# Graph attention and a graph convolution on one core: checks moved into the convolution, an end in written order, and outputs stored a block at a time

## The chip, the cores and the metric

The kernel runs on one core of one Trainium2 chip. The metric is the device time of one execution in microseconds. All data is in float32; some operands of TensorE are rounded to its own 32-bit form (fp32r).

## The reference, cut to what matters

```python
n, d = x.shape                      # 2708, 128
h = 8
q, k, v = ((x @ W.T).reshape(d, n, h) for W in (Wq, Wk, Wv))
a = jnp.einsum('dnh,dmh->dnm', q, k) * d ** -0.5
a = softmax(a + adj + adj, axis=2)
o = jnp.einsum('dnm,dmh->dnh', a, v).reshape(n, h * d) @ Wo.T
x = layernorm(x + o)
local_hidden = adj @ (x @ W2) + b2
local_cross = adj @ (local_hidden @ W4) + b4
embed = local_cross + local_hidden @ res_w.T + res_b
return layernorm(x + embed)
```

There are 128 heads of 8 channels over the same 2708 × 2708 matrix adj, so the attention has by far the most work. The layer normalisations are over the 128 features of a row and have no weights.

## The kernel before, in words

**Start and projections.** The first 256 rows of x and all three projection weights are loaded, and project_all makes the first queries, keys and values. The projections of the other rows are made in "quarters" that are strewn through the attention: load_quarter (L334, L336) loads a chunk of x (xc) and a quarter of a weight (wc), project (L344) multiplies them and hands the rest on as small jobs. The first of them, load_quarter(0), stands at L407, behind the first projections and the loads of the first group.

**Attention.** 32 groups of four heads; in a group six blocks of 452 query columns (the last has 448); in a block nine steps. A step makes scores on TensorE (L438), adds adj to most of them on VectorE (L445, tile e) and takes the exponential on ScalarE (L537). For one chunk of rows in each step the adjacency is not added ahead of the exponential: ScalarE takes the exponential of the bare scores (L534, tile w), and GpSimd multiplies it by exp(2·adj) (L535, tile ecol). exp(2·adj) is made once, in the first group, by first_exp: L418 on ScalarE, with accum_out, which sums each row beside the exponential, and L420 stores it to the buffers ne; later groups load it from there. In the last three groups look_at_near (L427) takes a minimum of each such tile. The products with the values add up in PSUM (L455, L460, L463); hand_on copies a block's sums out (L469) and stores them (L471, buffer os). The order of these steps on TensorE is written out by interleave, a planner with costs of its own for each step; loads run up to eight tiles ahead on SP's queue.

There is no maximum taken off before the exponentials. In its place the kernel checks that sums and factors lie within bounds, counts the partitions where they do in n_fine, and reads that number at the end; if a partition doesn't, a second form of the attention is run.

**End, first pass (layer0_out).** The weights and biases of the end are loaded first (L544 to L551). Then, for each of 22 chunks of 128 rows (the last has 20): load the head sums (ot, L587) and rows of x (xt, L589), two chunks ahead, in three buffers; reciprocal of the softmax sums (rd, L595); minimum and maximum of the sums for the check (reach, L598); product of all eight heads' sums with rd on VectorE (on, L600); eight transposes (pt, L603), a copy on ScalarE (oT, L605), eight products with Wo (py, L611), plus x (ys, L615), and mean and variance (statistics, L567 and L568). The chunks are taken in written order, with divide one chunk ahead of project and two ahead of add_x.

**End, second pass.** One root over the deviations of all chunks (L630), a reciprocal (L631), and then, four chunks at a time, normalise (L639), transpose (px, L641), copy (L646), multiply by W2 (pw, L649) and copy to xw (L651). The checks follow (L654 to L667).

**Layer 1.** Two passes over adj in six blocks of columns (five of 512 and one of 148), 22 tiles to a block. propagate loads a tile (col, L679, SP's queue, 24 buffers) and adds its product up in PSUM (acc, L680). In the first pass the sum plus b2 is lhT (L688), whose chunks are multiplied by W4 (ph, L691) and copied to hw (L692). In the second, a product with res_w is added (L683), the bias too (eT, L697), and for each chunk of 128 rows: transpose (pe, L700), plus x1 (y, L702), statistics, root, reciprocal, normalise (L574 to L577, tile xo), store (L705). This part has no written order: a scheduler decides where the instructions of one block stand among the loads and products of the next.

All loads and stores named here are issued by SP, in one order.

Of the kernel before, what the change touches and what calls it, by code (L numbers as in the profile page):

```python
# [18 lines left out]
P = 128  # L19
# [11 lines left out]
NEAR_LOW = 1e-30  # L31
NEAR_HIGH = 1e18
# [110 lines left out]
def graph_attention_gcn(ctx: ExitStack, tc: tile.TileContext, x, xT, adj, adjT, adjP, adjS,  # L143
# [42 lines left out]
    ends = const.tile([P, 2, len(QBS) * len(TWO_EXP)], F32, name="ends")  # L186


    with ExitStack() as s:
# [184 lines left out]
        for n in range(2):  # L374
            load_adj(n)

# [30 lines left out]
        load_quarter(0)  # L407
# [5 lines left out]
        def first_exp(b, m):  # L413

            nw = QBS[b][1]
            t = ecols.tile([P, QB], F32, tag="ecol", name="ecol")
            x = b * len(TWO_EXP) + TWO_EXP.index(m)
            nc.scalar.activation(t[:, :nw], adj_cols[0, b, -1 - m][:, :nw], AF.Exp, scale=2.0,  # L418
                                 accum_out=ends[:, 1, x : x + 1])
            nc.sync.dma_start(near_exp[b, m][:, :nw], t[:, :nw])  # L420
            exp_cols[0, b, m] = t

        def look_at_near(g, b, m):

            x = TWO_EXP.index(m)
            if x % 3 == g - NG + 3:
                nc.vector.tensor_reduce(ends[:, 0, ds(b * len(TWO_EXP) + x, 1)], exp_cols[g, b, m][:, : QBS[b][1]],  # L427
                                        AX.X, ALU.min)
# [51 lines left out]
        for what, n, c, beside in interleave(plan, len(steps) // len(plan), NU, amid, bufs=5):  # L480
# [14 lines left out]
            if c == 1 and jobs:  # L495
                jobs.pop(0)()
            if c == 0:
# [34 lines left out]
            if c == len(pieces) - 1:  # L532
                look_at_near(g, b, two)
                nc.scalar.activation(w[:, :, :nw], sp[:, :, :nw], AF.Exp, scale=2.0)  # L534
                nc.gpsimd.tensor_mul(w[:, :, :nw], w[:, :, :nw],  # L535
                                     exp_cols[g, b, two][:, :nw].unsqueeze(1).to_broadcast([P, 3, nw]))
                nc.scalar.activation(e[:, :at, :nw], e[:, :at, :nw], AF.Exp, scale=2.0)  # L537
# [5 lines left out]
    wo = keep.tile([P, H, D], F32, name="wo")  # L543
    nc.sync.dma_start(wo.rearrange("g e f -> g (e f)"), WoT)  # L544
    w2, w4, rw = (keep.tile([P, P], F32, name=f"w{i}") for i in range(3))
    for t, src in ((w2, W2), (w4, W4), (rw, res_wT)):
        nc.sync.dma_start(t, src)
    b2_sb, b4_sb, rb_sb, bias = (keep.tile([P, 1], F32, name=f"b{i}") for i in range(4))
    for t, src in ((b2_sb, b2), (b4_sb, b4), (rb_sb, res_b)):
        nc.sync.dma_start(t, src)  # L550
    nc.vector.tensor_add(bias, b4_sb, rb_sb)  # L551

# [8 lines left out]
    reach = keep.tile([P, 2, NM], F32, name="reach")  # L561
    nc.gpsimd.memset(reach, 1.0)
    fine = keep.tile([P, 5], F32, name="fine")
# [6 lines left out]
    def layernorm(to, y, w):  # L570
        mv = stat.tile([P, nc.vector.BN_AGGR_DIM], F32, tag="mv", name="mv")
        statistics(mv[:w], y, w)
        sd = stat.tile([P, 1], F32, tag="sd", name="sd")
        nc.scalar.activation(sd[:w], mv[:w, 1:2], AF.Sqrt, bias=eps[:w])  # L574
        rs = stat.tile([P, 1], F32, tag="rs", name="rs")
        nc.vector.reciprocal(rs[:w], sd[:w])
        nc.vector.tensor_scalar(to, y, mv[:w, 0:1], rs[:w], ALU.subtract, ALU.mult)  # L577

    def layer0_out(sb, ps, pa, judge):
# [4 lines left out]
        def load(c):  # L584
            i0, w = MC[c]
            ot = sb.tile([P, H + 1, P], F32, tag="ot", name="ot")
            nc.sync.dma_start(ot[:w], o3[ds(i0, w)])  # L587
            xt = sb.tile([P, D], F32, tag="xt", name="xt")
            nc.sync.dma_start(xt[:w], x[ds(i0, w), :])  # L589
            given[c] = ot, xt  # L590

        def divide(c):
# [3 lines left out]
            if judge:  # L596
                for i, op in enumerate((ALU.min, ALU.max)):
                    nc.vector.tensor_reduce(reach[:w, i, c : c + 1], ot[:w, H, :], AX.X, op)  # L598
            on = sb.tile([P, H, P], F32, tag="on", name="on")
            nc.vector.tensor_mul(on[:w], ot[:w, :H, :], rd[:w].unsqueeze(1).to_broadcast([w, H, P]))  # L600
# [16 lines left out]

        load(0)
        load(1)
        for c in range(NM + 2):  # L620
            if c + 2 < NM:
                load(c + 2)
# [4 lines left out]
            if c >= 2:  # L627
                add_x(c - 2)
        sd, rs = (sb.tile([P, NM], F32, tag=n, name=n) for n in ("sds", "rss"))
        nc.scalar.activation(sd, mvs[:, :, 1], AF.Sqrt, bias=eps)  # L630
        nc.vector.reciprocal(rs, sd)  # L631
        for c0 in range(0, NM, 4):
            cs = range(c0, min(c0 + 4, NM))
            px = pa.tile([P, 4, P], F32, tag="px", name="px")
            x1T = sb.tile([P, 4, P], F32, tag="x1T", name="x1T")
            pw = pa.tile([P, 4, P], F32, tag="pw", name="pw")
            for c in cs:
                w = MC[c][1]
                nc.vector.tensor_scalar(x1[:w, c, :], ys[:w, c, :], mvs[:w, c, 0:1], rs[:w, c : c + 1],  # L639
                                        ALU.subtract, ALU.mult)  # L640
                nc.tensor.transpose(px[:, c - c0, :w], x1[:w, c, :], ident[:w, :w])  # L641

            full = len([c for c in cs if MC[c][1] == P])
            parts = [(0, full, P)] + [(c - c0, 1, MC[c][1]) for c in cs if MC[c][1] < P]
            for i, n, w in parts:
                nc.scalar.copy(x1T[:, ds(i, n), :w], px[:, ds(i, n), :w])  # L646
            for c in cs:
                w = MC[c][1]
                nc.tensor.matmul(pw[:w, c - c0, :], x1T[:, c - c0, :w], w2, start=True, stop=True)  # L649
            for i, n, w in parts:  # L650
                nc.scalar.copy(xw[:w, ds(c0 + i, n), :], pw[:w, ds(i, n), :])  # L651
        if judge:
            finite = sb.tile([P, NM * D], F32, tag="finite", name="finite", bufs=1)
            nc.vector.tensor_scalar(finite, ys.rearrange("p c f -> p (c f)"), 0.0, 0.0, ALU.mult, ALU.is_equal)  # L654
            nc.vector.tensor_reduce(fine[:, 0:1], finite, AX.X, ALU.min)
            bounds = [(reach[:, 0, :], ALU.min, SUM_LOW, ALU.is_ge), (reach[:, 1, :], ALU.max, SUM_HIGH, ALU.is_le)]
            bounds += [(ends[:, 0, :], ALU.min, NEAR_LOW, ALU.is_ge), (ends[:, 1, :], ALU.max, NEAR_HIGH, ALU.is_le)]
            for i, (a, way, limit, op) in enumerate(bounds):
                end = keep.tile([P, 1], F32, name=f"end{i}")
                nc.vector.tensor_reduce(end, a, AX.X, way)  # L660
                nc.vector.tensor_scalar(fine[:, 1 + i : 2 + i], end, limit, None, op)
            every, ones = (keep.tile([P, 1], F32, name=n) for n in ("every", "ones"))
            nc.vector.tensor_reduce(every, fine, AX.X, ALU.min)
            nc.gpsimd.memset(ones, 1.0)
            pf = pa.tile([P, NB], F32, tag="py", name="pf", bufs=2)
            nc.tensor.matmul(pf[:1, :1], every, ones, start=True, stop=True)
            nc.vector.tensor_copy(n_fine, pf[:1, :1])  # L667

    def layer1(s, cols):
# [4 lines left out]
        def propagate(src, n0, nw, last=None):  # L674

            acc = ps.tile([P, NB], F32, tag="wide", name="acc1")
            for m, (m0, mw) in enumerate(MC):
                t = cols.tile([P, NB], F32, tag="col", name="col1")
                nc.sync.dma_start(t[:mw, :nw], adjT[ds(m0, mw), ds(n0, nw)])  # L679
                nc.tensor.matmul(acc[:, :nw], src[:mw, m, :], t[:mw, :nw], start=(m == 0),  # L680
                                 stop=(last is None and m == NM - 1))
            if last is not None:
# [3 lines left out]
        for n0, nw in NBS:  # L686
            acc = propagate(xw, n0, nw)
            nc.vector.tensor_scalar(lhT[:, ds(n0, nw)], acc[:, :nw], b2_sb, None, ALU.add)  # L688
            for i, w in chunks(nw, P):
# [4 lines left out]
        for n0, nw in NBS:  # L694
            acc = propagate(hw, n0, nw, (rw, lhT[:, ds(n0, nw)]))
            eT = sb.tile([P, NB], F32, tag="eT", name="eT")
            nc.vector.tensor_scalar(eT[:, :nw], acc[:, :nw], bias, None, ALU.add)  # L697
            for i, w in chunks(nw, P):
                pe = pa.tile([P, NB], F32, tag="narrow", name="pe")
                nc.tensor.transpose(pe[:w, :D], eT[:, ds(i, w)], ident)  # L700
                y = sb.tile([P, D], F32, tag="y", name="y1")
                nc.vector.tensor_add(y[:w], pe[:w, :D], x1[:w, (n0 + i) // P, :])  # L702
                o = sb.tile([P, D], F32, tag="xo", name="xo")
                layernorm(o[:w], y[:w], w)
                nc.sync.dma_start(out[ds(n0 + i, w), :], o[:w])  # L705

    def rest(judge):
        with ExitStack() as s:
            cols = s.enter_context(tc.tile_pool(name="cols1", bufs=24))
            with ExitStack() as t:  # L710
# [3 lines left out]
                t.enter_context(tc.manual_schedule())  # L714
                layer0_out(sb, ps, pa, judge)
            layer1(s, cols)
# [136 lines left out]
```

## Time and profile before

| | us |
|---|---|
| median of 3 runs | 6884.85 (6881.82 to 6886.79) |
| profiled execution | 6884.26 |
| its span | 6882.5 |
| start and projections | 0 to 62 |
| attention | 62 to 6543, some 201.5 for a group |
| end, first pass | 6543 to 6642.3 |
| end, second pass | 6642.3 to 6661.6 |
| layer 1, first pass | 6661.6 to 6764 |
| layer 1, second pass | 6764 to 6874.4 |
| tail | 6874.4 to 6882.5 |
| busy PE, DVE, ACT, POOL | 97%, 89%, 95%, 84% of the span |
| DMA | 1674 MB, 243 GB/s on average |

The profile is one execution of the program, with times from the start of its span; 1.8 us of the execution's own time lie outside the span. A row of the timeline gives the start, the time that it took, the engine, the line of the code, the operation, what it writes and reads, shapes and the number of instructions; in brackets stands how long the engine was idle before it and what it waited for. SPq, ACTq and so on are the instructions with which an engine issues a DMA. PE is TensorE's multiplication and PEld its loading of weights; DVE is VectorE, ACT ScalarE, POOL GpSimd.

### The profile page before, as it was taken

Reading aid. Unit: us, or ns where it says so; the run is one execution under the profiler, and the core shown is the slowest. Engines: PE = TensorE matmul, PEld = TensorE weight load, DVE = VectorE, ACT = ScalarE, POOL = GpSimd, SP = SyncE. Lnnn points to the kernel's source line nnn. Section 1 sums busy time; section 2 is a strip of 40 time slices with the busy share of each in tenths; the row PEclk is TensorE's granted clock in tenths of the full one; section 3 lists DMA queues with packets and bytes.
Section 4 is the critical chain, followed back from the end, with each engine's and each line's share of the span. In section 5 each row is a group of like instructions: output and inputs, shape, how many; then the busy total and the mean of one; then the engine's idle time right before and its main releaser. Section 6 shows DMA issues by size and latency. Waiting matters only on the chain.

```text
span 6882.5 us, 138849 instructions
## 1 busy us (share of the span) xinstructions
PE 6655.3 (97%) x50666; PEld 2002.7 (29%) x50666; DVE 6106.7 (89%) x6373; ACT 6505.4 (95%) x3659; POOL 5789.3 (84%) x2706
## 2 busy tenths in 40 slices
PE   7999999999999999999999999999999999999979
PEld 2222222222222222222222222222222222222254
DVE  6899999999999999999999999999999999999941
ACT  7999999999999999999999999999999999999910
POOL 5899988989888899998889999889898898888800
PEclk8999999999999999999999999999999999999999
DMA  8888888778888877788887778887788878777667
GB/s 254 261 250 250 249 244 248 243 246 250 249 254 245 239 245 244 246 251 252 246 243 248 244 240 250 242 253 243 248 251 247 249 233 239 243 233 230 193 204 233
DMA packets 1168590, 1674.27 MB, mean 243 GB/s; under 512 B 153982, under 2 KB 1135954, under 8 KB 1163802
## 3 DMA queue, kind: packets, MB, share of 16 engines
q1 hardware_dynamic: 1167642, 1664.50, 79.0%
q8 instruction: 402, 6.59, 0.4%
q14 instruction: 290, 2.38, 0.1%
q10 hardware_dynamic: 256, 0.81, 0.1%
HBM read 1582.90 MB, written 81.80 MB: 242 GB/s over the span
## 4 chain that ended last, share of the span: by engine, by line
PE 58%; DMA 11%; DVE 11%; POOL 6%; issue 5%; ACT 5%; SPq 4%; DVEq 0%; ACTq 0%; POOLq 0%
PE acc L463 29%; PE s L438 18%; DVE e L445 10%; POOL w L535 6%; DMA col<-in_adjP 4%; PE acc L680 3%; DMA two<-in_adjP 3%; ACT e L537 3%; PE p L438 2%; PE acc L455 2%; SPq L287 2%; ACT w L534 2%; DMA ecol<-ne 2%; PE s L344 1%; PE acc L460 1%
## 5 line engine op out<-in xcount | busy, mean ns | idle before, releaser
L535 POOL TENSOR_TENSOR w<-w,ecol 128x1356 f32<-128x1356 f32 (+1 forms) x1728 | 5347.8, 3102 | 696.1 <-ACT w L534 601.6
L445 DVE TENSOR_TENSOR e<-s,col 128x904 f32<-128x904 f32 (+1 forms) x4608 | 4817.2, 1091 | 320.6 <-PE s L438 130.3
L537 ACT ACTIVATE e<-e 128x2712 f32<-128x2712 f32 (+5 forms) x1728 | 4593.8, 2658 | 9.3 <-DVE e L445 4.3
L463 PE MATMUL acc<-e,vals 128*9 128x452 f32 x20352 | 3561.9, 545 | 0.4 <-ACT e L537 0.4
L438 PE MATMUL s<-q,k 32*128 32x452 f32 x10944 | 2475.2, 462 | 120.9 <-DVE e L445 93.3
L534 ACT ACTIVATE w<-p 128x1356 f32<-128x1356 f32 (+1 forms) x1728 | 2286.0, 1323 | 33.9 <-PE p L438 20.4
L438 PEld LDWEIGHTS s<-q,k 32*128 32x128 f32 x10944 | 997.6, 182 | 3267.6 <-DVE e L445 2845.5
L463 PE MATMUL acc<-w,vals 128*9 128x452 f32 x10368 | 1622.0, 544 | 0.0
L438 PE MATMUL p<-q,k 32*128 32x452 f32 (+1 forms) x5184 | 1328.1, 444 | 21.2 <-ACT w L534 19.6
L445 DVE TENSOR_TENSOR e<-s,two 128x904 f32<-128x904 f32 (+1 forms) x960 | 1048.3, 1092 | 126.5 <-PE s L438 81.3
L463 PEld LDWEIGHTS acc<-e,vals 128*9 128x9 f32 x20352 | 441.7, 88 | 786.2 <-issue 773.7
L438 PEld LDWEIGHTS p<-q,k 32*128 32x128 f32 x5184 | 547.1, 182 | 51.0 <-ACT w L534 45.3
L463 PEld LDWEIGHTS acc<-w,vals 128*9 128x9 f32 x10368 | 207.0, 88 | 175.8 <-issue 160.3
L262 POOL CAST k<-k_raw 128x336 fp32r<-128x336 f32 x251 | 222.2, 886 | 30.1 <-DMA q<-qs 30.1
L460 PE MATMUL acc<-e,v_first 128*32 128x452 f32 (+1 forms) x1536 | 188.9, 564 | 9.8 <-DVE o L469 2.0
L455 PE MATMUL acc<-e,v_short 128*128 128x452 f32 (+1 forms) x384 | 195.1, 590 | 0.0
L344 PE MATMUL s<-wc,xc 128*128 128x256 f32 (+1 forms) x480 | 166.4, 428 | 8.9 <-DMA wc<-in_WkT 7.5
L469 DVE COPY o<-acc 128x452 f32<-128x452 f32 x192 | 119.9, 624 | 40.0 <-PE acc L463 39.8
L360 POOL TENSOR_TENSOR pr<-pa,pr 128x256 fp32r<-128x256 f32 (+1 forms) x160 | 117.8, 736 | 12.8
L346 DVE TENSOR_SCALAR pa<-s 128x256 f32<-128x256 f32 (+1 forms) x240 | 100.2, 418 | 27.6 <-PE s L344 23.9
L344 PEld LDWEIGHTS s<-wc,xc 128*128 128x128 f32 (+1 forms) x480 | 70.5, 184 | 133.4 <-DVE e L445 116.4
L680 PE MATMUL acc<-col,xw 128*128 128x512 f32 (+2 forms) x264 | 106.0, 551 | 0.0
(85 smaller groups left out, 1041.6 us busy)
## 6 DMA issues: line engine op xcount, KB each, us to landing
col<-in_adjP SPq DMA_DIRECT2D x1965, 226.0 KB
two<-in_adjP SPq DMA_DIRECT2D x1440, 226.0 KB
ecol<-ne SPq DMA_DIRECT2D x1395, 226.0 KB
col<-in_adjP SPq DMA_DIRECT2D x393, 224.0 KB
two<-in_adjP SPq DMA_DIRECT2D x288, 224.0 KB
ecol<-ne SPq DMA_DIRECT2D x279, 224.0 KB
col<-in_adjT SPq DMA_DIRECT2D x210, 256.0 KB
k_raw<-ks SPq DMA_DIRECT2D x504, 84.6 KB
```

The source lines that it names most:

```text
L262: copy(k[:, :, ts(i, n)], t[:, ts(i, n * NU)].rearrange("p (q c) -> p c q", c=NU))
L287: queues[i].dma_start(q[ds(32 * j + 2 * H * i, 2 * H), :nw].bitcast(F32), qs[:, ds((GB * g + j) * N + n0, nw)])
L344: nc.tensor.matmul(pp[:mi, 0, :QW], given[c][:, :mi], given.pop((c, i, h)), start=True, stop=True)
L438: nc.tensor.matmul(to[:, :nw], k[r, m, :], q[r], start=True, stop=True)
L445: nc.vector.tensor_add(e[:, ds(at, 2), :nw], st[:, :, :nw], a)
L455: nc.tensor.matmul(a[:, :nw], vz, e[:, t, :nw], start=False, stop=False)
L460: nc.tensor.matmul(a[ds(32 * j, 32), :nw], v_first[g % 2][:, ds(32 * j, 32)], e[:, t, :nw], start=True, stop=False)
L463: nc.tensor.matmul(a[ds(32 * j, VW), :nw], v[:, m, ds(VW * j, VW)], e[:, t, :nw], start=False, stop=(m == last_chunk))
L534: nc.scalar.activation(w[:, :, :nw], sp[:, :, :nw], AF.Exp, scale=2.0)
L535: nc.gpsimd.tensor_mul(w[:, :, :nw], w[:, :, :nw], exp_cols[g, b, two][:, :nw].unsqueeze(1).to_broadcast([P, 3, nw]))
L537: nc.scalar.activation(e[:, :at, :nw], e[:, :at, :nw], AF.Exp, scale=2.0)
L680: nc.tensor.matmul(acc[:, :nw], src[:mw, m, :], t[:mw, :nw], start=(m == 0), stop=(last is None and m == NM - 1))
```

## The change

- load_quarter(0) moves to the first loads of the kernel.
- first_exp loses accum_out, and look_at_near goes. The check on the factors is made on adj itself: in the first pass of layer 1 VectorE takes the largest absolute value of each tile (132 of them).
- The weights wo, w2 and the biases are loaded 40 steps before the attention's end; w4 and rw after the first three loads of the end.
- layer0_out: ot has four buffers and xt six, loads run three chunks ahead; the reach reductions go; the product "on" is split, five heads on VectorE and three on GpSimd; roots, normalisation, transposes and the product with W2 are made for four chunks at a time within the pass.
- All of the end is in written order (manual_schedule). In it the work that follows a block (form_hw; put_out) is kept in a list and taken when the next block has loaded its tile 3 or 6.
- The checks (verdict) are made in block 0 of the second pass of layer 1, at its tile 6, from the stored sums (os, loaded once more) and the largest values; their count at tile 3 of block 1.
- Outputs: a block's four chunks are transposed into one PSUM tile, with one sum y, one root, one reciprocal, four normalisations and one store. Of block 0 this is done at tile 6 of block 1, of the others at tile 3 of the next block.

The diff, cut to its core:

```diff
@@ -373,6 +383,7 @@
         for n in range(2):
             load_adj(n)
+        load_quarter(0)
...
             project_all(1, i)()
-        load_quarter(0)
...
-            nc.scalar.activation(t[:, :nw], adj_cols[0, b, -1 - m][:, :nw], AF.Exp, scale=2.0,
-                                 accum_out=ends[:, 1, x : x + 1])
+            nc.scalar.activation(t[:, :nw], adj_cols[0, b, -1 - m][:, :nw], AF.Exp, scale=2.0)
...
+            if n == len(steps) - 40 and c == 0:
+                load_weights()
...
-                look_at_near(g, b, two)
...
-            ot = sb.tile([P, H + 1, P], F32, tag="ot", name="ot")
+            ot = sb.tile([P, H + 1, P], F32, tag="ot", name="ot", bufs=4)
...
-            if judge:
-                for i, op in enumerate((ALU.min, ALU.max)):
-                    nc.vector.tensor_reduce(reach[:w, i, c : c + 1], ot[:w, H, :], AX.X, op)
             on = sb.tile([P, H, P], F32, tag="on", name="on")
-            nc.vector.tensor_mul(on[:w], ot[:w, :H, :], rd[:w].unsqueeze(1).to_broadcast([w, H, P]))
+
+            for multiply, e, n in ((nc.gpsimd.tensor_mul, 5, 3), (nc.vector.tensor_mul, 0, 5)):
+                multiply(on[:w, ds(e, n), :], ot[:w, ds(e, n), :], rd[:w].unsqueeze(1).to_broadcast([w, n, P]))
...
+        for c in range(NM + 4):
+            if c + 3 < NM:
+                load(c + 3)
             if c < NM:
                 divide(c)
             if 0 <= c - 1 < NM:
                 project(c - 1)
-            if c >= 2:
+            if stage2:
+                form_xw(*stage2)
+                stage2 = None
+            if 0 <= c - 2 < NM:
                 add_x(c - 2)
+            if stage1:
+                stage2 = stage1[0], normalise(*stage1)
+                stage1 = None
+            if c - 2 in steps_of:
+                stage1 = steps_of[c - 2], deviations(steps_of[c - 2])
...
+        def propagate(src, n0, nw, last=None, look=False):
 
             acc = ps.tile([P, NB], F32, tag="wide", name="acc1")
             for m, (m0, mw) in enumerate(MC):
                 t = cols.tile([P, NB], F32, tag="col", name="col1")
                 nc.sync.dma_start(t[:mw, :nw], adjT[ds(m0, mw), ds(n0, nw)])
+                if m in (3, 6) and due:
+                    due.pop(0)()
                 nc.tensor.matmul(acc[:, :nw], src[:mw, m, :], t[:mw, :nw], start=(m == 0),
                                  stop=(last is None and m == NM - 1))
+                if look:
+                    x = n0 // NB * NM + m
+                    nc.vector.tensor_reduce(ends[:mw, x : x + 1], t[:mw, :nw], AX.X, ALU.max, apply_absolute_value=True)
...
+            acc = propagate(xw, n0, nw, look=judge)
+            take_lh(acc, n0, nw)
+            due.append(lambda n0=n0, nw=nw: form_hw(n0, nw))
+        if judge:
+            due.append(lambda: due.append(verdict(sb, pa)))
...
+        def put_out(eT, n0, nw):
...
+            for i, (at, x) in enumerate(chunks(nw, P)):
+                nc.tensor.transpose(pe[:x, i, :], eT[:, ds(at, x)], ident)
...
+            for i, k, x in parts:
+                nc.vector.tensor_add(y[:x, ds(i, k), :], pe[:x, ds(i, k), :], x1[:x, ds(c0 + i, k), :])
+            for i, (at, x) in enumerate(chunks(nw, P)):
+                statistics(mv[:x, i, :], y[:x, i, :], x)
+            for i, k, x in parts:
+                nc.scalar.activation(sd[:x, ds(i, k)], mv[:x, ds(i, k), 1], AF.Sqrt, bias=eps[:x])
+            for i, k, x in parts:
+                nc.vector.reciprocal(rs[:x, ds(i, k)], sd[:x, ds(i, k)])
+            for i, (at, x) in enumerate(chunks(nw, P)):
+                nc.vector.tensor_scalar(o[:x, i, :], y[:x, i, :], mv[:x, i, 0:1], rs[:x, i : i + 1], ALU.subtract, ALU.mult)
+            for i, k, x in parts:
+                nc.sync.dma_start(out[ds(n0 + i * P, k * x), :].rearrange("(c p) f -> p c f", p=x), o[:x, ds(i, k), :])
+
+        for n0, nw in NBS:
+            acc = propagate(hw, n0, nw, (rw, lhT[:, ds(n0, nw)]))
+            eT = take_e(acc, n0, nw)
+            due.append(lambda eT=eT, n0=n0, nw=nw: put_out(eT, n0, nw))
+        while due:
+            due.pop(0)()
...
         with ExitStack() as s:
+            s.enter_context(tc.manual_schedule())
             cols = s.enter_context(tc.tile_pool(name="cols1", bufs=24))
```

## The prediction

> **What bounds the kernel now.** I read the busy time by stretch first, to see which engine a stage has none to spare of, then the order of instructions at the places that the change touches. The columns are PE, PEld, DVE, ACT and POOL busy, granted clock, DMA share and GB/s.
>
> ```profile
> 64.40:267.50 203.10, 184.18 (x1339) 52.80 (x1339) 167.66 (x166) 203.08 (x193) 162.40 (x77) 0.97 0.87 267
> 1000.00:3000.00 2000.00, 1963.91 (x15340) 564.34 (x15336) 1849.47 (x1868) 1989.88 (x1071) 1800.15 (x847) 1.00 0.81 247
> 6342.00:6543.00 201.00, 189.73 (x1499) 52.06 (x1499) 181.06 (x189) 193.13 (x103) 160.74 (x52) 0.97 0.61 195
> ```
>
> In the attention stage ACT is busy for 203.08 of 203.10 us in the first group and 1989.88 of 2000 in the middle: what shortens ACT's work shortens the stage, and what shortens only DVE's does not. The last group shows 7.9 us without ACT. The end (6543 to 6882.5) has no work for ACT: its first part waits for loads and DVE, then PE is busy without a gap (110.37 of 110.40 us in the second layer-1 pass).
>
> **What the Trainium skill says.** "SBUF — State Buffer", Who interferes with whom: a DVE instruction with two SBUF inputs contends with a GpSimd one that reads SBUF, and the first of the two holds the port for its whole instruction. The trace agrees: the cast of L262 takes POOL 0.87 to 0.89 us alone and 1.23 beside a DVE cast; DVE 0.51 alone, 1.17 to 1.18 beside POOL. "TensorE: Matmul & The Clock Gate", Part 1: The HAM clock gate: after idling for some us PE runs at half clock for a few. The trace agrees: the same eight transposes took 1.94 us at 6601.10, in a half-clock stretch, and 1.06 at 6565.09. "DMA: Bandwidth & Descriptors", Anatomy of one DMA — SWDGE (gpsimd) path: "any semaphore wait happens on the issuing sequencer before dispatch", not in the DMA engines. The section is on GpSimd's path and these transfers are issued by SP, but the trace agrees for SP: the last fence shows it.
>
> **The start (faster).** load_quarter(0) moves from behind the projections to the first loads.
>
> ```profile
> 50.57 1.24 SPq L336 DMA_DIRECT2D wc<-in_WkT  x1
> 53.28 0.19 ACT L418 ACTIVATION_READ_ACCUMULATOR ecol<-col 128x1 f32 x1
> 54.91 1.19 PE L344 MATMUL s<-wc,xc 128*128 128x256 f32 x2 [7.48 <-DMA wc<-in_WkT]
> 61.45 1.30 ACT L534 ACTIVATE w<-p 128x1356 f32<-128x1356 f32 x1 [7.98 <-PE s L438]
> ```
>
> PE sits idle for 7.48 us for a weight that was issued at 50.57, and ACT for 7.98. With the weight there since about 4 us, the scores that end ACT's gap come 7.5 earlier, at 54.0 for an ACT that is free at 53.5. ACT has no slack in what follows, so it lasts: **7 us** (5 to 8). The two issues cost SP 1.2 us ahead of 11 us in which it does nothing.
>
> **accum_out of L418.** ACT spends 0.47 us on the exponential and then reads an accumulator; the next instruction starts 0.56 us after the exponential did (49.47, 49.94, 50.03). Without the read 0.09 us go, 54 times: **5 us** (4 to 5.5), all on ACT.
>
> **look_at_near.** 54 reductions of 0.61 us, 33 us of DVE in the last three groups. But those groups take 201.0 to 201.6 us against 201.5 in the others: DVE was not what ended them. Only two ACT gaps in the last group (2.85 and 1.36 us) may close: **2 us** (0 to 4). Moved loads of weights, off-path: nothing; SP has room in that group (DMA share 0.61).
>
> **The first pass of the end.** 22 chunks, then the second pass, which goes into the first.
>
> ```profile
> 6567.21 0.95 DVE L595 RECIPROCAL rd<-ot 128x128 f32<-128x128 f32 x1 [1.53 <-DMA ot<-os]
> 6568.08 0.41 DVE L598 TENSOR_REDUCE reach<-ot 128x1 f32<-128x128 f32 x2
> 6568.41 1.22 DVE L600 TENSOR_TENSOR on<-ot,rd 128x1024 f32<-128x1024 f32 x1
> 6569.55 0.28 DVE L615 TENSOR_TENSOR ys<-py,xt 128x128 f32<-128x128 f32 x1
> 6569.78 1.06 PE L603 MATMUL pt<-ident,on 128*128 128x128 f32 x8 [1.84 <-DVE on L600]
> ```
>
> Before: first reciprocal at 6553.02, last aggregate at 6642.26: 89.2 us or 4.05 a chunk, 15.0 of it in ten waits of DVE for an ot load. Then comes the second pass; the first layer-1 pass ran as if from 6657.3. After: (1) the weight loads that stood ahead of ot (6545.06 to 6548.30) are gone and the first ot load stands where it did relative to the os stores: 5.2 us earlier, so a first reciprocal at about 6547.8. (2) With four ot buffers and loads three ahead the 15 us of waits go: a load takes 4.6 to 4.9 us and then has over 7. (3) A chunk costs DVE 0.9 reciprocal + 0.75 (five heads of the 1.22 us product) + 0.3 + 0.3 + 0.2 for y and statistics + 0.3 normalise, 2.8 in all; PE 0.9 + 1.85 + 0.4 for px and pw, 3.1. (4) POOL's share: three heads, 384 of the 1356 elements that take it 3.10 us in L535: 1.03 us. If it ran beside DVE, PE would bound: 22 × 3.1 + 15 to fill and drain gives a start of pass 1 at 6631. With the port lock, 0.75 and 1.03 stand in line and "on" comes 1.8 us after rd, longer than the 1.22 it took; DVE's next reciprocal is not held, but the chain is: 3.5 to 3.8 us a chunk. I take the lock: 22 × 3.65 + 10 from 6547.8 is 6638. Against 6657.3: **18 us** (12 if POOL goes first; 26 without the lock). The column loads, which fill 24 buffers from about 6606 at 0.68 us each, are there by 6632: just in time.
>
> **Checks in layer 1.** A look at each of 132 tiles: DVE 0.61 × 512/452 = 0.69 us beside PE's 0.86 (four products at 0.43); it hides, DVE being busy for 3.9 of 102.4 us there. The other checks, about 11 us of DVE and 1.39 MB for the sums, lie in pass 2, block 0, where DVE is busy for 22.8 of 110 us and 24 tiles lie ready. If that cover were gone, up to 15 us. Four ph at once on two buffers: 0.4 × 5 = **2 us lost**.
>
> **The stores in pass 2 (slower).** Here lies the loss. Before, the first store of a block stood on SP behind 18 or more of the next block's column loads:
>
> ```profile
> 6805.73 1.88 PE L680 MATMUL acc<-col,hw 128*128 128x512 f32 x4
> 6807.45 0.38 PE L700 MATMUL pe<-ident,eT 128*128 128x128 f32 x2
> 6808.74 7.46 PE L680 MATMUL acc<-col,hw 128*128 128x512 f32 x17
> 6809.77 1.51 SPq L705 DMA_DIRECT2D out<-xo  x3
> 6811.37 0.79 SPq L679 DMA_DIRECT2D col<-in_adjT  x2
> ```
>
> SP issues no column load from 6805.9 to 6811.37, because it waits for xo, but PE runs on over tiles that are loaded (17 products without a pause). After, in the order of SP's instructions, out of block b stands behind only **four** column loads of block b+1 (seven in block 1), and PE reaches the put_out that it waits for when one tile of those is left. So all 24 buffers are run dry each time. From the first transpose: transposes 0.65, y over 512 elements 0.69, four bn_stats with bn_aggr 1.8, root 0.36, reciprocal 0.2, four xo 1.1: the store is issued at +4.9, the next column load at +5.4, and lands 2.75 us later by 6811.37 to 6814.12 (up to 3.3 behind a 256 KB store): +8.65. PE has done its last tile at +1.3. Stall 7.4 us. Then PE is in half clock for some 5 us, worth 2.3. **9.7 × 4 blocks = 39 us**; in the last, 148 wide, SP issues 18 loads at 0.475 us against PE's 0.25 a tile: **10 us**. In all **49 us** (40 to 56). What ends the stall next is the load's latency; nothing covers it.
>
> **Sum.** −7 −5 −2 −18 +2 +49 = +19 us on the profiled execution's 6884.3 (span 6882.5 and 1.8 around it), which is 0.6 under the median of the runs: **6904**.
>
> **Rivals.**
> - The gains cancel the stalls (21%): POOL's product runs beside DVE's (−26 instead of −18) and PE keeps full clock (7.4 × 4 + 10 = 40): −14 −26 + 2 + 40 = +2, 6887. For it: the casts of L262 are another form than the product. Against it: a broadcast of rd still reads SBUF twice.
> - Faster (7%): SP's store doesn't hold the column loads. One mechanism: the lead that PE has in loaded tiles when it reaches put_out. The chain of 8.65 us is 10 tiles of 0.86; with a lead of ten or more after the store there's no stall, and −32 + 2 gives 6855. Against it: SP has one queue, and its order has four loads.
> - Larger loss (12%): POOL takes the port first (−12), first tiles after each pause land 1.5 us apart, as they did after 6792 in part: 56 lost. −14 −12 + 2 + 56 = +32, 6917.
> - That the change doesn't do what it says: only for the checks, whose DVE work was no bound; it is in the first sums.
>
> **The numbers.** The forecast has 60%, with 6894 to 6914 as its own range from the ranges of its terms. The low end of the full range lies inside the cancelling case, the high end inside the larger loss: 6882 to 6918. What a measurement of this kernel can tell from no change is 0.2%, 13.8 us: 6871 to 6898.6. Slower: five sixths of the forecast (0.50) and the larger loss (0.12), 0.62. Same: the rest of the forecast (0.10) and the cancelling case (0.21), 0.31. Faster: 0.07.
>
> **What would show it.** In the profile after: no 7.48 us wait of PE for wc; no ACTIVATION_READ_ACCUMULATOR; groups of 201.5 us as before outside the first; chunks of 3.65 us with POOL's product beginning when DVE's ends; five idle stretches of PE of 7 to 10 us in pass 2, each ended by a column load, and SP waiting on out's xo just before. Wrong would be: PE in pass 2 without gaps (then faster), or chunks over 4 us.

## The result, and the profile after

The changed kernel takes 6921.05 us (median of 5 runs, 6917.98 to 6921.59), the kernel before 6884.85 (5 runs in the same comparison, 6881.82 to 6887.05). The ratio is 1.0048, 95% interval 1.0038 to 1.0059: some 33 us slower by the ratio (36 by the medians), where 19 were forecast and the range ended at 6918. The profiled execution took 6917.98 us, its span 6916.0, so the two profiles lie 33.5 us apart by span. These 33.5 us can be laid out by stage. The cuts are the same four events in both kernels: the first score, the last hand_on of the first group and of the attention, and the sums lhT and eT of the first and last blocks of layer 1. For each stage its length before and after:

| stage | before | after | difference | forecast |
|---|---|---|---|---|
| start, to the first score | 41.3 | 45.7 | +4.4 | |
| group 0 of the attention | 250.0 | 252.5 | +2.5 | −12 |
| groups 1 to 28 | 5648.1 | 5650.4 | +2.3 | 0 |
| groups 29 to 31 | 603.6 | 599.8 | −3.8 | −2 |
| end: first pass, second pass, block 0 of layer 1 | 133.7 | 108.6 | −25.1 | −18 |
| layer 1, pass 1, blocks 1 to 5 | 87.6 | 89.7 | +2.1 | +2 |
| layer 1, pass 2 | 110.1 | 161.2 | +51.1 | +49 |
| tail | 8.1 | 8.3 | +0.2 | 0 |

(The forecast's 7 us for the wait for wc fall between the first score and the end of group 0; its 5 for accum_out in group 0 too.)

The largest entry is pass 2. Here is the timeline of the changed kernel at the first output store, in block 1:

```profile
6772.90 0.60 PE L738 MATMUL pe<-ident,eT 128*128 128x128 f32 x4
6773.34 1.02 PE L699 MATMUL acc<-col,hw 128*128 128x512 f32 x2
...
6776.66 1.11 DVE L750 TENSOR_SCALAR xo<-y,mv,rs 128x128 f32<-128x128 f32 x4
6777.80 0.40 SPq L752 DMA_DIRECT2D out<-xo  x1
6778.31 11.09 SPq L696 DMA_DIRECT2D col<-in_adjT  x19
6781.34 15.85 PE L699 MATMUL acc<-col,hw 128*128 128x512 f32 x30 [6.98 <-DMA col<-in_adjT]
```

From the transposes at 6772.90 PE has one tile left (two matmuls, 1.02 us). SP issues the store at +4.9, the first column load behind it at +5.4, and PE starts again at +8.44, after 6.98 us of waiting for a column. Before, seventeen matmuls (eight tiles and a half) ran on at this place. The waits of SP in pass 2 of the changed kernel (engine and line, what it waited for, us in total, times, longest) name the cause:

```profile
SPq L752 <- DVE xo L750: 70.0, 5, 16.7
SPq L696 <- DMA col<-in_adjT: 16.1, 53, 0.7
SPq L696 <- PE acc L699: 8.7, 27, 1.4
```

SP stands before the five stores for 70.0 us, and for all that time it issues no load. Of those 70 us PE feels what its lead doesn't cover: "PE acc L699 <- DMA col<-in_adjT: 35.4, 7, 7.0", 35.4 us in seven waits. The rest of the 51 is mostly the clock. Two stretches show it, from PE's restart to the end of the half clock and the time after it (start and end, length, then PE, PEld, DVE, ACT and POOL busy, granted clock, DMA share, GB/s):

```profile
6781.34:6786.44 5.10, 5.10 (x6) 2.16 (x7) 0.00 (x0) 0.00 (x0) 0.00 (x0) 0.50 1.02 369
6786.44:6796.00 9.56, 9.56 (x23) 3.99 (x21) 0.00 (x0) 0.00 (x0) 0.00 (x0) 1.00 0.69 251
```

Busy time by stretch in the changed kernel, the first pass of the end, pass 1 and pass 2, in the same columns:

```profile
6553.00:6635.30 82.30, 74.25 (x595) 68.10 (x595) 62.59 (x142) 30.36 (x41) 35.02 (x23) 0.94 0.81 236
6635.30:6746.60 111.30, 110.59 (x306) 52.34 (x306) 71.44 (x135) 5.25 (x22) 0.00 (x0) 0.98 0.76 227
6746.60:6907.70 161.10, 125.55 (x302) 57.23 (x302) 33.14 (x86) 2.01 (x7) 0.00 (x0) 0.87 0.54 187
```

In pass 2 the 302 matmuls take 125.5 us, where pass 2 before had PE busy for 110.4 at full clock. The 15 us more come with the half clock behind the gaps (five stretches like the first line above, worth 13 of them), and 125.5 + 35.4 is the stage's 161. In pass 1 VectorE is now busy for 71.4 us with the looks at the tiles, and PE doesn't wait for it (110.59 of 111.30).

In the start of the changed kernel PE no longer waits for wc, but VectorE and ACT wait for something else, a little later:

```profile
4.04 0.45 SPq L346 DMA_DIRECT2D wc<-in_WkT  x1
...
51.77 1.22 PE L354 MATMUL s<-wc,xc 128*128 128x256 f32 x2
...
62.54 2.11 DVE L446 TENSOR_TENSOR e<-s,col 128x904 f32<-128x904 f32 x2 [3.30 <-DMA col<-in_adjP]
...
65.16 0.58 ACT L427 ACTIVATE ecol<-col 128x452 f32<-128x452 f32 x1 [3.00 <-DMA col<-in_adjP]
```

And in the first pass of the end the product is split as written, with PE behind it:

```profile
6569.85 0.82 DVE L583 TENSOR_TENSOR on<-ot,rd 128x640 f32<-128x640 f32 x1
6569.95 1.58 POOL L583 TENSOR_TENSOR on<-ot,rd 128x384 f32<-128x384 f32 x1 [1.69 <-DVE rd L579]
6570.82 1.31 PE L586 MATMUL pt<-ident,on 128*128 128x128 f32 x8
6571.97 1.95 PE L594 MATMUL py<-wo,oT 128*128 128x128 f32 x16
```

POOL begins when VectorE does and takes 1.58 us; by the row of the prediction (3.10 us for 1356 elements) its 384 elements are worth 0.88. 1.58 is VectorE's 0.82 less the 0.10 that POOL starts later, plus 0.86. That fits what the Trainium skill states in "SBUF — State Buffer", Who interferes with whom: one of the two holds the port and the other stands still for all of that instruction.

### The profile page after: what moved, and what is told of

The parts are those of the page before. It is cut to its first block, busy times and chain, and to the rows that moved or that the text cites. A ratio compares the mean times of both kernels' runs of the same rounds, so it can differ in the third digit from the quotient of the medians.

```text
span 6916.0 us, 138800 instructions
## 1 busy us (share of the span) xinstructions
PE 6681.8 (97%) x50666; PEld 2013.6 (29%) x50666; DVE 6145.7 (89%) x6380; ACT 6497.1 (94%) x3595; POOL 5823.4 (84%) x2728
## 4 chain that ended last, share of the span: by engine, by line
PE 62%; DVE 12%; DMA 8%; ACT 7%; issue 6%; POOL 3%; SPq 3%; DVEq 0%; ACTq 0%; POOLq 0%
PE acc L464 31%; PE s L439 20%; DVE e L446 11%; ACT e L539 4%; POOL w L537 3%; PE acc L699 3%; ACT w L536 3%; DMA two<-in_adjP 3%; PE p L439 3%; DMA col<-in_adjP 2%; PE acc L456 2%; SPq L297 1%; PE s L354 1%; PE s L436 1%; PE acc L461 1%
## 5 line engine op out<-in xcount | busy, mean ns | idle before, releaser
L539 ACT ACTIVATE e<-e 128x2712 f32<-128x2712 f32 (+5 forms) x1728 | 4655.5, 2694 | 13.6 <-DVE e L446 9.2
L536 ACT ACTIVATE w<-p 128x1356 f32<-128x1356 f32 (+1 forms) x1728 | 2348.1, 1359 | 29.2 <-PE p L439 25.3
L699 PE MATMUL acc<-col,hw 128*128 128x512 f32 (+2 forms) x264 | 118.7, 604 | 35.4 <-DMA col<-in_adjT 35.4
```

## The experiments

Each ratio is to the kernel before in the same comparison, with its 95% interval; the medians of the kernel before there were 6887.02 to 6888.12 us.

**1. The early load alone.** The kernel before, with one edit:

```diff
         for n in range(2):
             load_adj(n)
+        load_quarter(0)
...
             project_all(1, i)()
-        load_quarter(0)
```

> The kernel before with one edit: load_quarter(0) among the first loads. Theory of the prediction (PE's 7.48 us wait is the only thing between the two stretches of ACT): 7 us faster than before, about 6878. Theory formed from the profile after (the DMA queues are nearly full from 16 to 100 us, so that the wait only covered others, and the key loads of the start take 1.24 us each in place of 0.83): no gain, 0 to 8 us slower, 6885 to 6893, with first scores at about 45.7 us in place of 41.3.

Measured: 6887.46 us, ratio 0.9997 (0.9989 to 1.0005): no gain by the median. The interval reaches just over 7 us, so the trace has to decide: the first scores come at 41.95 us, and group 0 takes 251.1 us (250.0 before), no shorter. Two stretches of the kernel before (the first fence) and of this one (the second) show where the 7.5 us went:

```profile
45.00:64.00 19.00, 10.88 (x61) 3.60 (x59) 8.55 (x10) 10.09 (x10) 8.94 (x9) 0.58 1.05 321
64.00:100.00 36.00, 32.55 (x231) 8.93 (x226) 30.67 (x31) 36.00 (x36) 26.82 (x11) 0.98 0.92 273
```

```profile
45.00:64.00 19.00, 16.18 (x88) 4.92 (x88) 13.14 (x14) 16.48 (x16) 14.62 (x14) 0.72 0.99 294
64.00:100.00 36.00, 30.71 (x211) 8.17 (x209) 26.76 (x28) 31.17 (x31) 22.43 (x10) 0.86 0.96 291
```

To 64 us ACT does 6.4 us more than before (16.48 against 10.09), and to 100 us it loses 4.8 of them again (31.17 against 36.00), with the DMA share at 0.96. Its waits there are for col and two, the loads of adj. Over all of group 0 ACT's idle time, summed from the gaps between its instructions, is 10.4 us in the kernel before (7.98 of it the gap that the prediction saw) and 10.8 here (the gap is 0.62). The wait for wc was only one of several limits; without it the loads of adj are late.

**2. The checks on the factors alone.** The kernel before without accum_out and look_at_near.

```diff
-            nc.scalar.activation(t[:, :nw], adj_cols[0, b, -1 - m][:, :nw], AF.Exp, scale=2.0,
-                                 accum_out=ends[:, 1, x : x + 1])
+            nc.scalar.activation(t[:, :nw], adj_cols[0, b, -1 - m][:, :nw], AF.Exp, scale=2.0)
...
-                look_at_near(g, b, two)
```

> The kernel before without accum_out in the exponential of the factors and without the minima of the factors in the last three groups; left out is the check on the factors, its bounds are given ones. Theory of the prediction (ACT bounds the first group): 5 us from the first group and 2 to 4 from the last three, 6876 to 6878. Rival (the first group is held by DMA as soon as ACT has slack): only the last three groups gain, 2 to 4 us, 6881 to 6883, and ACT shows waits for DMA in the first group.

Measured: 6879.49 us, ratio 0.9990 (0.9983 to 0.9996): 7 us faster. Most comes from the last three groups: 595.8 us where the kernel before takes 603.6. Group 0 takes 249.4 (250.0 before). ACT's work in it, its length less its gaps, falls from 239.6 to 235.4 us, as the 54 reads of 0.09 us said, but its gaps grow from 10.4 to 14.0. So the gain has the size of the prediction's case (7 to 9 us), its places are the rival's.

**3. The early load taken out of the changed kernel.** load_quarter(0) back at its old place, the rest as changed.

> The changed kernel with load_quarter(0) put back behind the first projections. If the early load is what delays the start: first scores back at about 41.3 us, 4 to 7 us faster than the changed kernel, 6914 to 6917. If the start's delay comes from something else in the change (where tiles lie in memory, say), no difference, 6921.

Measured: 6913.73 us, ratio 1.0041 (1.0027 to 1.0054), not told apart from the changed kernel's 1.0048 (1.0038 to 1.0059). The first scores come at 46.1 us, so the early load isn't what delays the start. ACT's gap is back (9.96 us), and group 0 takes 249.3 us, no longer than with the early load.

**4. The stores on another queue.** The changed kernel with

```diff
-                nc.sync.dma_start(out[ds(n0 + i * P, k * x), :].rearrange("(c p) f -> p c f", p=x), o[:x, ds(i, k), :])
+                nc.scalar.dma_start(out[ds(n0 + i * P, k * x), :].rearrange("(c p) f -> p c f", p=x), o[:x, ds(i, k), :])
```

> The changed kernel with the output stores issued by ACT in place of SP, at the same places; ACT has nothing else to do there. If the stores hold the column loads on SP's queue, pass 2 of layer 1 goes from 161 us back to 110 to 113, no wait of PE for a column is left, and the kernel takes 6921 - 50 = 6871 (6868 to 6876). If PE waits for another reason (the DMA engines, the column buffers), the gaps of 7 us stay and it takes 6915 to 6921.

Measured: 6865.56 us, ratio 0.9969 (0.9957 to 0.9981): faster than both kernels. Pass 2 takes 110.6 us, and its stretch shows PE busy throughout at full clock:

```profile
6742.80:6853.40 110.60, 110.49 (x302) 51.10 (x302) 33.17 (x86) 2.00 (x7) 0.00 (x0) 1.00 0.78 268
```

The arithmetic ahead of the stores, their size and their place in the program are unchanged. What is gone is SP's wait on xo.

**5. Five tiles of lead in place of one.** The changed kernel with the store, still SP's, behind four more column loads; put_out now returns its stores as a job, which is taken there:

```diff
...
+                now[0] = m
                 if m in (3, 6) and due:
                     due.pop(0)()
+                if stores and stores[0][0] == m:
+                    stores.pop(0)[1]()
...
-            due.append(lambda eT=eT, n0=n0, nw=nw: put_out(eT, n0, nw))
+            due.append(lambda eT=eT, n0=n0, nw=nw: stores.append((now[0] + 4, put_out(eT, n0, nw))))
```

> The changed kernel with each output store, still SP's, put behind four more column loads; the arithmetic ahead of it stays where it is. If the lead in loaded tiles decides, PE has five tiles in place of one when the chain to the store starts: it works until 4.8 us after its start in place of 1.3, the next column lands at 8.4, so the gaps are 3.5 to 4 us in place of 7, and pass 2 takes 133 to 137 us in place of 161: 6893 to 6898. If the store's own transfer is what delays, the gaps stay: 161 us, 6921.

Measured: 6898.98 us, ratio 1.0018 (1.0011 to 1.0025); pass 2 takes 144.4 us. The gaps are as expected (3.3 to 3.5 us in the four wide blocks), the stage is 7 us longer than the upper end. One of the gaps in the timeline, the waits and the stretch of pass 2:

```profile
6799.42 14.32 PE L702 MATMUL acc<-col,hw 128*128 128x512 f32 x28 [3.33 <-DMA col<-in_adjT]
```

```profile
PE acc L702 <- DMA col<-in_adjT: 20.0, 6, 5.7
```

```profile
6742.00:6886.00 144.00, 123.64 (x301) 55.76 (x299) 32.69 (x86) 2.01 (x7) 0.00 (x0) 0.91 0.60 207
```

The waits fall from 35.4 to 20.0 us. But PE is still busy for 123.6 us: a gap of 3.3 to 3.5 us costs nearly as much half clock as one of 7. The expectation had left that out.

**6. Eleven tiles of lead.** The same, ten loads later in place of four.

> The changed kernel with each output store, still SP's, put behind ten more column loads. The lead of eleven tiles lasts PE 9.9 us from the start of the chain, the next column lands at 8.4: no gap and no half clock in the four wide blocks; in the last, whose tiles take 0.25 us, a gap of 4 to 6 us remains. Pass 2 of layer 1 in 115 to 120 us, the kernel at 6870 to 6876. If any store on SP's queue costs a gap, 140 us and more.

Measured: 6872.52 us, ratio 0.9978 (0.9969 to 0.9988); pass 2 takes 116.7 us, with one wait of PE for a column left, 4.2 us in the last, narrow block. So it isn't the store on SP's queue that costs, but a store that PE's lead doesn't outlast: 161, 144 and 117 us with one, five and eleven tiles, and 111 with the stores on another queue.

**7. Where the tiles lie.** In all runs of the kernels with the changed attention stage the start is late (first scores at 44.4 to 46.7 us). The kernel before with an unused tile in SBUF:

```diff
+    shift = const.tile([P, 1180], F32, name="shift")
```

> The kernel before with an unused tile of 1180 floats a partition ahead of the attention's tiles, so that these lie in SBUF where the changed kernel has them. Found so far: with the changed kernel's layout (three runs) a key load takes 1.24 us and the first scores come at 45 to 46 us, with the layout of before (three runs) 0.83 to 1.0 and 41.3 to 42. If where the tiles lie does it, first scores at 45 to 46 here. If not, 41 to 42.

Measured: 6891.09 us, ratio 1.0005 (0.9996 to 1.0014), first scores at 41.9 us. The place in SBUF alone doesn't do it.

**8. A pad in the changed kernel.** As in experiment 4, with an unused tile of 100 floats.

> The changed kernel with its stores issued by ACT and 100 unused floats a partition ahead of the attention's tiles, which puts them at the same place as before in steps of 1024 bytes. If the key loads depend on a tile's place within such a step, first scores at 41 to 42 us and 6861; else 45 and 6866 as without the pad.

Measured: 6861.72 us, ratio 0.9964 (0.9950 to 0.9978), the lowest median of all, but not told apart from experiment 4 by the intervals. First scores at 44.4 us, a key load every 1.18 us: the pad does nothing that can be seen.

**9. No share for GpSimd.** As in experiment 4, with the product of all eight heads on VectorE:

```diff
-            for multiply, e, n in ((nc.gpsimd.tensor_mul, 5, 3), (nc.vector.tensor_mul, 0, 5)):
+            for multiply, e, n in ((nc.vector.tensor_mul, 0, H),):
```

> The changed kernel with its stores issued by ACT and the product of all eight heads on VectorE, none on GpSimd. Theory after the profile: PE bounds a chunk (57.2 of 60 us busy), and GpSimd's part waits for VectorE's anyway (1.58 us where the row of L537 gives 0.88 for as many elements), so the pass takes the same within 3 us or is 1 to 3 us shorter: 6863 to 6869. Rival (the split does pay): 22 times the 0.4 us that VectorE is longer, 9 us more, 6875.

Measured: 6866.11 us, ratio 0.9971 (0.9961 to 0.9980), the same as experiment 4. From the attention's end to the first lhT it takes 109.4 us (108.4 with the split). The stretch of 60 us in the middle of the first pass, in the changed kernel and in this one:

```profile
6562.00:6622.00 60.00, 57.18 (x485) 53.38 (x484) 49.41 (x114) 24.60 (x31) 28.51 (x18) 1.00 0.80 227
```

```profile
6562.00:6622.00 60.00, 54.18 (x473) 52.23 (x472) 54.94 (x110) 24.15 (x31) 0.00 (x0) 1.00 0.77 221
```

With the split PE is busy for 57.2 of 60 us; without it PE and VectorE for 54 to 55 each. The split moves VectorE away from the bound and PE takes its place: worth about 1 us.

**10. Fewer bytes in the first group.** As in experiment 4, without the stores of the factors; the later groups load rows of adj in their place, so this kernel's attention isn't the reference's.

```diff
-            nc.sync.dma_start(near_exp[b, m][:, :nw], t[:, :nw])
...
-                nc.sync.dma_start(t[:, :nw], near_exp[b, -1 - m][:, :nw])
+                nc.sync.dma_start(t[:, :nw], adjP[ds((-1 - m) * P, P), ds(n0, nw)])
```

> The changed kernel with its output stores issued by ACT; left out are the 54 stores of the factors in the first group (12 MB, some 34 us of all DMA engines), and the later groups load adj itself in their place, as many bytes. If the first group is held by DMA once ACT has slack, it takes 237 to 241 us in place of 248 to 252, and the kernel 6855 to 6858. If not, 248 to 252 and 6862 to 6866.

Measured: 6862.52 us, ratio 0.9963 (0.9949 to 0.9977). Group 0 takes 245.1 us, between the two expectations; the other kernels with the changed attention take 247.9 to 252.5. ACT's gaps in it are 9.0 us against 11 to 16. So DMA seems to be a part of what holds the first group, some 3 to 7 us of it, not all; this rests on one profiled execution of each kernel, and the time of the whole kernel isn't told apart from that of experiment 4.

**11. All edits of the attention at once, in the kernel before.** Experiments 1, 2 and 7 together.

> The kernel before with all that the change does ahead of the end at once: load_quarter(0) first, no checks on the factors (left out), and tiles shifted by 4720 bytes. Each alone left the first scores at 41.3 to 42 us. If it is the sum that delays the start, 44 to 46 us; if it comes from elsewhere in the program, 41 to 43. Time of the kernel 6878 to 6883 either way.

Measured: 6881.76 us, ratio 0.9991 (0.9982 to 1.0000). First scores at 44.8 us: with all three the start is late, with each alone it wasn't. Group 0 takes 247.9, groups 29 to 31 take 595.7.

**12. Deeper loads alone.** The kernel before with four buffers for ot, six for xt, and loads three chunks ahead.

```diff
-            ot = sb.tile([P, H + 1, P], F32, tag="ot", name="ot")
+            ot = sb.tile([P, H + 1, P], F32, tag="ot", name="ot", bufs=4)
...
-            if c + 2 < NM:
-                load(c + 2)
+            if c + 3 < NM:
+                load(c + 3)
```

> The kernel before with four buffers for the head sums and loads three chunks ahead; the weight loads, the reach reductions, the whole product on VectorE and the second pass stay. From the attention's end to the first sum of layer 1 the kernel before takes 131 to 134 us, the changed one 108 to 109. If the waits of VectorE for head sums (15.0 us) were the larger part of that, 12 to 15 us go here: 118 to 121, 6873 to 6876. If PE or VectorE take their place, fewer than 8.

Measured: 6870.45 us, ratio 0.9975 (0.9965 to 0.9985). From the attention's end to the first lhT it takes 117.1 us, 17 less than before and 1 less than the lower end of the first case expected. Of the 25 us that the changed kernel gains at the end, two thirds are this one edit; the lot of the other edits there (weights loaded early, no reach, normalisation within the pass, the split) share 8 to 9, some 5 of it the weights (below).

## Why the prediction was right or wrong

**Right: the sign and its cause.** The stores in pass 2 were forecast at 49 us and cost 51. The mechanism was the stated one, in its order: SP stands before the store, the 24 buffers are run dry, the chain to the next column takes 8.44 us (8.65 forecast), the gap is 6.8 to 7.0 in the wide blocks (7.4). Experiment 4 takes away only the wait on SP, and 50.6 us go; experiments 5 and 6 let the lead grow, and the gaps shrink by as much. Two terms inside were off and cancel, which is luck for the 49: the gaps came to 35.4 us (forecast 39.6), the rest to 15 us (forecast 9.2 of half clock, 2.3 for each of four gaps). The clock's records show half clock for 6.8 to 10.2 us at each of five gaps, but they begin 1.7 to 4.7 us before PE starts again. PE itself works at half clock for 4.8 to 5.9 us behind a gap, close to the prediction's 5, and loses 2.4 to 2.9; there are five such gaps, and the prediction counted none of it in the last, narrow block. That is 13 of the 15 us; the other 2 were not traced further.

**Right: the hidden costs.** The looks at 132 tiles cost nothing but what was stated for the four ph at once (+2.1 in pass 1, forecast +2): the 40 products for ph hold PE for 6.6 us from each one's start to the next instruction's, 4.6 before. The checks in pass 2 cost nothing either (110.6 us in experiment 4, with them in it).

**Wrong: the start and the first group.** This step failed as the prediction put it: "ACT has no slack in what follows, so it lasts". Experiment 1 has that edit alone and gains nothing. ACT's 100% was true with the 8 us of delay. Without it the loads of adj are late, and ACT gets gaps of 1 to 3 us from 58 us on; that they had caught up during the delay is the likely reading, with experiment 10 for it in part. The prediction's own first line shows a DMA share of 0.87 for the group, and the stretches of experiment 1 show 1.05 and 0.92 at its start; what DMA would do if ACT came earlier wasn't asked. The 5 us of accum_out are gone from ACT's work (239.6 to 235.4), and group 0 is hardly shorter for it: ACT's gaps grow instead. The group takes 247.9 to 252.5 us with any mix of the edits that keeps the stores of the factors. In place of −12 the first group gave +2.5, between executions that differ by 2 to 4 us among kernels with the same attention.

**Wrong by 4 us, and not settled: the late start.** The key loads ahead of the first scores took 0.83 to 1.01 us each in the five kernels without the full set of edits, and 1.16 to 1.24 in all that have both the checks gone and the tiles moved. In the records of the changed kernel the eight packets of a load start within 0.4 us of each other and take 1.21 us each, in the kernel before they are more spread and take 0.84. Neither the early load (experiments 1 and 3) nor the shift (7) nor the checks (2) does it alone, and all three together do (11). The checks gone and the tiles moved, without the early load, were run in the changed kernel only (experiment 3: 46.1 us), and why this acts on loads at 16 us was not found.

**Right in direction, too small: the end's first pass.** 25 us in place of 18. The first term was right: the first reciprocal comes 4.8 us after the attention's last hand_on, 10.0 before, so 5.3 us earlier (forecast 5.2). The mis-sized term is the time per chunk, forecast at 3.65 us for a chain through the port lock; it came to 3.27, nearer the 3.1 that the prediction had for PE alone. The lock was there (POOL 1.58 us), but the chain wasn't the bound: the transposes of VectorE's five heads begin before POOL is done, and PE is the bound, with 57.2 of 60 us busy. From the first reciprocal at 6553.0 to the first product of layer 1 at 6635.3 it took 82 us, forecast 90. The rival "POOL beside VectorE" (26 us) came nearer the number for a reason that the runs contradict. (Slips in the sums mattered little: POOL's share is 0.88 us by the row used, not 1.03; 6657.3 less 6638 is 19, not 18; a tile of 512 columns is two products of 0.43 us, not four.)

**Too small: look_at_near. Wrong: the moved weights at nothing.** Forecast were 2 us from two gaps of ACT, and "nothing" for the early loads of the weights. Groups 29 to 31 take 602 to 605 us in the four kernels with the minima, and 595.7 to 595.8 in the two that drop them and leave the weights where they were (experiments 2 and 11): 6 to 9 us. In the eight kernels that move the weights too they take 598 to 600, so 2 to 4 us are lost again. They are lost in one block of the last group, which takes 36.6 to 38.1 us in those eight and 33.4 in the two. In it, shortly after the weights are loaded, VectorE adds two biases, 128x1 each; in the kernel before it did so behind the attention. The changed kernel (first fence) and the kernel before (second):

```profile
6393.78 3.08 POOL L537 TENSOR_TENSOR w<-w,ecol 128x1356 f32<-128x1356 f32 x1 [0.45 <-ACT w L536]
6393.91 2.96 DVE L545 TENSOR_TENSOR b<-b,b 128x1 f32<-128x1 f32 x1
...
6397.94 0.75 PE L439 MATMUL s<-q,k 32*128 32x452 f32 x2 [2.54 <-DVE e L446]
...
6403.82 1.30 ACT L536 ACTIVATE w<-p 128x1356 f32<-128x1356 f32 x1 [2.36 <-PE p L439]
```

```profile
6550.31 0.16 DVE L551 TENSOR_TENSOR b<-b,b 128x1 f32<-128x1 f32 x1 [6.70 <-DMA b<-in_res_b]
```

The sum takes 0.16 us while GpSimd is idle. Here it ends with GpSimd's product, 2.96 us later, as the port lock would have it that the prediction used for the end's first pass, in a place where it didn't look. PE and ACT wait behind it, ACT for 3.8 us in this block, where experiment 11 shows no wait. No run has the sum moved without the loads, so the cause is read from the trace alone.

The sum, on the two profiled executions: of the attention's 14 us 1.3 came (+2.5 and −3.8), 12.7 didn't; 4.4 of start, 2.3 of scatter in groups 1 to 28 and 2.1 in pass 2 came on top, 7.1 more were gained at the end, and some tenths in pass 1 and the tail. 19 + 12.7 + 4.4 + 2.3 + 2.1 − 7.1 is 33.4. The −3.8 are themselves look_at_near's 6 to 9 less the 2 to 4 of the moved weights. The median of the runs is 3 us above the profiled execution, and 3 us above the range.

## What to carry to other kernels

A wait in a queue of loads costs what the lead in loaded data doesn't cover: count the loads that stand ahead of a store on its queue, not the buffers, and put a store that waits for arithmetic on a queue that nobody waits for (here some 55 us for one word). An engine that is 100% busy isn't proof that its savings last; look at what the stage's second-busiest resource would do if the engine came earlier, above all right after a stall that let that resource catch up. When work is moved from one engine to another, find which engine bounds the step first: moving three eighths of the product to GpSimd gave about nothing, loads one chunk further ahead gave 17 us. And when loads move, look at what waits for them: here a small sum came along with them into a stage where GpSimd is busy.

## What was not expected of the hardware

- The clock's loss hardly grows with the gap in this range. Four gaps of PE of 3.3 to 3.5 us and one of 5.7 (experiment 5) left PE busy for 123.6 us in pass 2, five gaps of 6.7 to 7.0 for 125.5, no gaps for 110.5. PE worked at half clock for 3.4 to 6.1 us behind the former and for 4.8 to 5.9 behind the latter. "TensorE: Matmul & The Clock Gate", Part 1: The HAM clock gate, of the Trainium skill puts the idle window at about 3.4 us. The traces don't show that length as a threshold: a gap of 3.34 us was followed by half clock, and so were two of 2.15 and 1.99 us in the first pass of the kernel before (from 6598.95 and 6611.72, half clock from 6601.03 and 6614.68), while gaps of 1.6 to 1.9 us there were not.
- A sum of two 128x1 tiles on VectorE took 0.16 us with GpSimd idle, in six kernels, and 2.95 to 2.97 us in the eight kernels where a GpSimd product of 3.1 us had begun 0.12 to 0.14 us before it.
- Eight-row loads from the key buffer took 0.83 to 1.01 us each in some kernels and 1.16 to 1.24 in others, with the same bytes and the same queues.
